# A four-layer selective scan on one core: instruction order in the scan stage taken from the source, with two steps issued one unit later

## The chip, the core and the metric

The kernel runs on one core of a Trainium2 chip. The core has five engines that run side by side: TensorE (PE, matrix multiplication), VectorE (DVE), ScalarE (ACT), GpSimd (POOL) and SyncE (SP), which here issues all the transfers between the chip's main memory and the core's own memory. An engine works through its own list of instructions and waits on semaphores for what other engines have to deliver. PE writes to PSUM[...]; everything else lies in the on-chip memory SBUF. The metric is the device time of one execution in microseconds (us). One execution was also taken by the profiler; all times by instruction come from it.

## The reference, cut to what matters

Four layers follow one another on eight images of 48 x 48 positions and 96 channels. Each adds to its input the result of a two-dimensional selective scan:

```
x = x + ss2d(groupnorm(x))          # four times, with different weights
ss2d: xz = x @ in_proj;  xc, z = halves of xz            # 192 channels each
      xc = silu(depthwise_conv3x3(xc))
      for each of 4 directions k (rows, columns, and both reversed), L = 2304 positions:
          dts, B, C = x_proj[k] @ xc                      # ranks 6 or 16, 16 states, 16 states
          delta = softplus(dt_proj[k] @ dts + bias)
          h[n]  = exp(delta * A[n]) * h[n] + delta * xc * B[n]      # along L, for n in 0..15
          y    += sum over n of h[n] * C[n]
      out = (layernorm(y) * silu(z)) @ out_proj
```

Layer 3 writes its scan as cumulative sums and a division by a decay. When the decay has faded to nothing, only the first and last positions matter, and the kernel computes just these ("short"), with a full second pass held in reserve.

## The kernel before, in words

**Tiling.** Two images form a pair, four pairs a layer, so layers 0 to 2 have twelve pairs. The 192 channels of both images are laid into three tiles of 128 partitions (t = 0 and 1 hold 128 channels of one image each, t = 2 the last 64 of both). A *group* is one tile t, one phase ph (rows or columns) and one direction d: twelve groups to a pair. A group's 2304 positions are scanned in three *chunks* of 768, each for 16 states n. One state of one chunk is a *unit*: 48 to a group, 576 to a pair, 6912 in layers 0 to 2.

**A unit**, in the class `Chunk`, has five steps:

- `load` (L518): SP fetches the row C[n], repeated over the partitions, into one of seven `cb` buffers, and for n = 0 also the rows of B (`brow`).
- `decay` (L537): ACT computes exp(delta * A[n]) into one of four `da` buffers (L543).
- `spread` (L548): PE spreads the row B[n] over the partitions into one of two PSUM tiles `b` (L558).
- `scan` (L562): DVE multiplies `b` by delta * u (L570) and scans (L574), in place in `da`. Unless the chunk is the last, ACT copies the last column of the scan into `carry` (L585), where the same state of the next chunk starts. Then POOL multiplies `cb` by the scan (L586).
- `add_up` (L588): PE adds `cb` into the single accumulator `acc` (L593). After n = 15 `collect` (L600) lets DVE add `acc` into y (L609, L614 or L619). At the end of a tile y is stored (L623).

**Side work.** Three generators are advanced in between, one step at a time, each step ending at a `yield`:

- `prepare` (L417) makes delta and delta * u of the next group, in five pieces of 480 or 384 positions. A piece has six steps: load of `dts` (L433); matmul and three ACT operations (L444 to L453); three ACT operations (L456 to L459); two POOL operations on `lg` (L461, L462); one DVE operation (L464); an ACT copy and a DVE product (L466, L468 or L470).
- `prologue` (L234) is the front end of the next pair: load of x (L310), group norm, input projection (L345, L352), the convolution as nine matmuls with diagonal weights per piece, three to a step (L258), silu with its table loads (L223, L224), x_proj (L395, L399), the store of its result (L411), and `split` (L270), which cuts it into three bf16 parts and stores them (L275 to L282). Its buffers `parts` and `rest` exist once.
- `epilogue` (L728) is layer norm, gate and output projection of the pair before, in 16 pieces of ten steps.

**The order of the work.** `run` (L839) writes one turn of a loop for each unit k: get_ready(k+1), which is load(k+3), decay(k+2) and spread(k+1); scan(k); one step of `prepare`; one step of `prologue` in the last third of a pair, or one of `epilogue` every second turn before that; add_up(k-3). This is the order of the source only. A planner inside the framework then decides the order in which each engine gets its instructions: it plays the program through with its own estimates of durations, and gives each engine, among the instructions that it takes to be ready, the one that stands first in the source. An instruction whose input it thinks late is passed by later ones. On the chip each engine keeps to the order that came out.

**Weights of a layer.** When a layer's first prologue begins, the constructor of `Layer` loads the weights and derives small tables from them (L178 to L197). `make_diag` (L200) then writes 18 diagonal matrices on DVE (L205), all at once.

Of the kernel before, what the change touches and what calls it, by code (L numbers as in the profile page):

```python
# [32 lines left out]
BF16 = mybir.dt.bfloat16  # L36
AF = mybir.ActivationFunctionType
ALU = mybir.AluOpType

P = 128  # L40
NB, H, W, DM = 8, 48, 48, 96
# [51 lines left out]
def ss2d_layers_kernel(ctx: ExitStack, tc: tile.TileContext, x_in, consts, weights, out):  # L93
    nc = tc.nc
# [47 lines left out]
    for b in range(2):  # L142
# [3 lines left out]
            mybir.AxisListType.X,  # L146
            ALU.add,
        )
# [7 lines left out]
    nc.vector.tensor_reduce(  # L156
        mine, ident.rearrange("p (b q) -> p b q", b=2), mybir.AxisListType.X, ALU.add
    )
# [4 lines left out]
    class Layer:  # L163


        def __init__(self, l):
            self.l = l
            self.rank = r = RANKS[l]
            self.nx = nx(r)
            cols, n = weight_columns(r)  # L170
            wt = wpool.tile([P, n], F32, name=f"w_{l}", tag="w")
            nc.sync.dma_start(wt, weights[l])
            part = {k: wt[:, a:b] for k, (a, b) in cols.items()}
            self.inw = part["inw"][0:DM]
            self.xp = part["xp"].rearrange("p (t f m) -> p t f m", t=2, f=2)
            self.dtw = part["dtw"].rearrange("p (k d) -> p k d", k=4)
            self.outw = part["outw"].rearrange("p (t c) -> p t c", t=2)
            self.outw_2 = wpool.tile([P, 2, DM], F32, name=f"outw2_{l}", tag="outw2")  # L178
            for b in range(2):
                nc.vector.tensor_scalar_mul(  # L180
                    self.outw_2[:, b, :], self.outw[:, 1, :], mine[:, b : b + 1]
                )
            self.par = part["par"].rearrange("p (t c) -> p t c", t=2)

            self.a = wpool.tile([P, 2, 4 * NS], F32, name=f"a_{l}", tag="a")
            nc.scalar.activation(self.a, self.par[:, :, C_ALOG : C_ALOG + 4 * NS], AF.Exp)
            nc.vector.tensor_scalar_mul(self.a, self.a, -1.0)

            self.amax = wpool.tile([P, 2, 4], F32, name=f"amax_{l}", tag="amax")
            nc.vector.tensor_reduce(  # L190
                self.amax, self.a.rearrange("p t (k n) -> p t k n", n=NS),
                mybir.AxisListType.X, ALU.max,
            )
            self.dsum = wpool.tile([P, 2], F32, name=f"dsum_{l}", tag="dsum")
            nc.vector.tensor_reduce(
                self.dsum, self.par[:, :, C_D : C_D + 4], mybir.AxisListType.X, ALU.add
            )  # L197
            self.diag = None

        def make_diag(self):  # L200

            self.diag = dpool.tile([P, 2, 9, P], F32, name=f"diag_{self.l}", tag="diag")
            for t in range(2):
                for j in range(9):
                    nc.vector.tensor_scalar_mul(  # L205
                        self.diag[:, t, j, :], ident, self.par[:, t, C_CONVW + j : C_CONVW + j + 1]
                    )

        def column(self, t, c):
            return self.par[:, int(t == 2), c : c + 1]  # L210
# [22 lines left out]

    def prologue(l, p, short=False):  # L234
        ly = layers[l]
        if ly.diag is None:
            ly.make_diag()
        gn = sm2.tile([DM, 2, 2], F32, name=f"gn_{l}_{p}", tag="gn")
        xd = dram.tile([2, 2, ly.nx, L], F32, name=f"xd_{l}_{p}", tag=f"xd{ly.rank}")
        xb = dram.tile([2, 2, PARTS, 3 * NS, L], BF16, name=f"xb_{l}_{p}", tag="xb")  # L240
# [4 lines left out]
        def padded(name):  # L245
            pad = tmp.tile([P, H + 2, W + 2], F32, name=name, tag="tmp")
            nc.gpsimd.memset(pad[:, 0 : H + 2 : H + 1, :], 0.0)
            nc.gpsimd.memset(pad[:, 1 : H + 1, 0 : W + 2 : W + 1], 0.0)
            return pad
# [20 lines left out]
        def split(xt, c0, m, to):  # L270
# [13 lines left out]
                )  # L284
            yield

        pad2 = padded(f"pad2_{l}_{p}")
        for b in range(2):
            x = tmp.tile([DM, L], F32, name=f"x_{l}_{p}_{b}", tag="tmp")
# [43 lines left out]
            nc.scalar.activation(scale, scale, AF.Exp, scale=-0.5)  # L333
            nc.vector.scalar_tensor_tensor(shift, mg, -1.0, scale, ALU.mult, ALU.mult)
            yield
# [165 lines left out]
    def picked(t, n):  # L501
# [2 lines left out]
            return 2 * NR, pick2[:, n, :]  # L504
        return NR, pick[:, n : n + 1].to_broadcast([NR, P])

    class Chunk:


# [52 lines left out]
        def scan(self, n):  # L562
            s, m = state[self.l, self.p], self.m
            way = (lambda z: z) if self.d == 0 else (lambda z: z[:, ::-1])
            _, du = s["dd", self.t, self.ph, self.d]
            carries = self.group["carry"]
            start = 0.0 if self.first else carries[:, n : n + 1]
            da, c = self.da.pop(n), self.cb[n][:, :m]
            b = self.b.pop(n)[:, :m]
            nc.vector.tensor_mul(b, du[:, self.c0 : self.c0 + m], b)  # L570
            if self.l < NLAYER - 1:

                h = da
                nc.vector.tensor_tensor_scan(way(h), way(da), way(b), start, ALU.mult, ALU.add)  # L574
            else:

                h = self.rq.pop(n)
                nc.vector.tensor_mul(b, h, b)
                nc.vector.tensor_tensor_scan(
                    way(h), ones.to_broadcast([P, m]), way(b), start, ALU.mult, ALU.add  # L580
                )
                nc.gpsimd.tensor_mul(c, c, da)
            if not self.last:
                end = m - 1 if self.d == 0 else 0
                nc.scalar.copy(carries[:, n : n + 1], h[:, end : end + 1])  # L585
            nc.gpsimd.tensor_mul(c, c, h)  # L586

        def add_up(self, n):  # L588
            if n == 0:
                self.acc = pacc.tile([P, 2 * BANK], F32, name="acc", tag="acc")  # L590
            c = self.cb.pop(n)
            for z, zm in pieces(self.m):
                nc.tensor.matmul(  # L593
                    self.acc[:, z : z + zm], ident, c[:, z : z + zm],
                    start=(n == 0), stop=(n == NS - 1),
                )
            if n == NS - 1:
                self.collect()

        def collect(self):  # L600

# [23 lines left out]
    class Edge:  # L625
# [68 lines left out]
        def add_up(self, i):  # L694
            if i == 0:
                self.acc = pacc.tile([P, 2 * BANK], F32, name="acc", tag="acc")
            c = self.cb.pop(i)
            for j in range(QUAD):
                nc.tensor.matmul(  # L699
                    self.acc[:, :EDGE], ident, c[:, j, :],  # L700
                    start=(i == j == 0), stop=(QUAD * i + j == NS - 1),
                )
            if QUAD * i + QUAD == NS:
                self.collect()

        def collect(self):
            l, p, t, s = self.l, self.p, self.t, state[self.l, self.p]
# [118 lines left out]
    def drain(g):  # L826
        for _ in g:
            pass

    def step(g, n=1):  # L830
        for _ in range(n):
            if next(g, StopIteration) is StopIteration:
                return

    groups = [(t, ph, d) for t in range(3) for ph in range(2) for d in range(2)]
    LAG = 3
    LOADS, DECAYS = 2, 1

    def run(pairs, short):  # L839
# [40 lines left out]
        drain(begin(*pairs[0]))  # L880
        drain(prepare(*pairs[0], *groups[0], pairs[0][0] in short))
        behind = ahead = coming = iter(())
        get_ready(0)
        for k, ((l, p, gi, j), c, n) in enumerate(todo):
            at = pairs.index((l, p))
            following = pairs[at + 1] if at + 1 < len(pairs) else None
            per = NS // QUAD if l in short else len(SCANS) * NS
            unit = gi * per + j

            after = 2 * len(groups) * per // 3  # L890
            if unit == after:
                drain(behind)
                if following:
                    ahead = begin(*following)
            if j == 0:
                drain(coming)
                if gi + 1 < len(groups):
                    coming = prepare(l, p, *groups[gi + 1], l in short)
                elif following:
                    drain(ahead)  # L900
                    coming = prepare(*following, *groups[0], following[0] in short)
                else:
                    coming = iter(())
            if j == max(0, per - 1 - LOADS - DECAYS):
                drain(coming)
            get_ready(k + 1)
            c.scan(n)
            step(coming)
            if unit >= after:
                step(ahead, 8 if l in short else 1)  # L910
            elif l in short:
                step(behind, 6)
            elif unit % 2 == 0:
                step(behind)
            if k >= LAG:
                todo[k - LAG][1].add_up(todo[k - LAG][2])
                (bl, bp, bgi, bj) = todo[k - LAG][0]
                if todo[k - LAG + 1][0][:2] != (bl, bp):
                    behind = epilogue(bl, bp)
        for (_, c, n) in todo[-LAG:]:  # L920
            c.add_up(n)
        drain(epilogue(*pairs[-1]))

    last = NLAYER - 1
    run([(l, p) for l in range(NLAYER) for p in range(NPAIR)], (last,))


    every = sm1.tile([P, 1], F32, name="every", tag="every")
# [102 lines left out]
```

## Time and profile before

| | |
|---|---|
| time, median of 3 runs | 25900.11 us (25893.95 to 25902.8) |
| span of the profiled execution | 25882.9 us |
| PE busy | 20983.2 us (81%) |
| DVE busy | 20922.0 us (81%) |
| POOL busy | 15340.0 us (59%) |
| ACT busy | 13772.3 us (53%) |
| DMA engines, mean share | 40.2% |

A row for a group of instructions gives the line, the engine, the operation, what it writes and reads, its shape and count; after the first bar the busy time in all and the mean of one in ns; after the second bar the time for which the engine stood idle just before such instructions, and the instruction whose end released it. A row of waits reads: who waited, for whom, us in total, how often, the longest. In the timeline the first number is the start in us, the second how long the instruction, or several alike in a row (x2, x4), took. A busy share is an average over stages that have different limits, so the stages of one pair are looked at apart.

### The profile page before, as it was taken

To read this page: it belongs to the slowest core of one execution; us is meant where nothing else is said; L and a number is where in the kernel's file an instruction comes from. 1 tells how busy PE (TensorE), PEld (TensorE's weight loads), DVE (VectorE), ACT (ScalarE), POOL (GpSimd) and SP (SyncE) were. 2 spreads that over 40 slices of the span, in tenths; PEclk is the share of its full clock that TensorE was granted. 3 is DMA by queue.
4 is the path that set the end of the run, shared out by engine and by line. 5 is a ranking of instruction groups with operands and counts; after the bars stand their busy time and mean duration, and the time that the engine had idled before them with its cause. 6 is when DMAs were issued, how large, how long until landed. Compare 5 with 4: busy or idle time off the path is not lost. (4 is left out here: it accounts for less than half of the span.)

```text
span 25882.9 us, 233918 instructions
## 1 busy us (share of the span) xinstructions
PE 20983.2 (81%) x64962; PEld 9542.0 (37%) x64962; DVE 20922.0 (81%) x18566; ACT 13772.3 (53%) x22878; POOL 15340.0 (59%) x9545
## 2 busy tenths in 40 slices
PE   7787887887887887887887887887887887887886
PEld 2333333333333333333333333333333333334555
DVE  5888888988888988988988988988888988887443
ACT  4454554554554554554554554554554554555775
POOL 4656656656666656656656656656656656655332
PEclk8898898998898898898898998898898998898886
DMA  2344444434434444434434444444434434444221
GB/s 90 126 122 130 132 123 127 134 119 130 134 120 132 135 121 133 134 121 134 134 121 131 134 122 130 134 121 130 134 119 132 134 120 130 132 122 115 64 62 50
DMA packets 1463442, 3150.92 MB, mean 122 GB/s; under 512 B 190832, under 2 KB 563696, under 8 KB 1448944
## 3 DMA queue, kind: packets, MB, share of 16 engines
q1 hardware_dynamic: 1462128, 3135.85, 40.2%
q8 instruction: 525, 8.60, 0.1%
q14 instruction: 789, 6.46, 0.1%
HBM read 2971.05 MB, written 164.07 MB: 121 GB/s over the span
## 5 line engine op out<-in xcount | busy, mean ns | idle before, releaser
L586 POOL TENSOR_TENSOR cb<-cb,da 128x768 f32<-128x768 f32 x6912 | 12427.8, 1809 | 7755.9 <-DVE da L574 4843.6
L593 PE MATMUL acc<-cb,cst 128*128 128x512 f32 (+1 forms) x27648 | 12228.8, 568 | 2394.0 <-POOL cb L586 2114.9
L543 ACT ACTIVATE da<-dl,a 128x768 f32<-128x768 f32 x6912 | 6448.9, 935 | 7878.0 <-POOL cb L586 7851.1
L570 DVE TENSOR_TENSOR b<-du,b 128x768 f32<-128x768 f32 x6912 | 6481.8, 951 | 2488.9 <-PE b L558 2461.6
L574 DVE TENSOR_TENSOR_SCAN da<-da,carry,b 128x768 f32<-128x768 f32 x4608 | 8182.2, 1801 | 90.0 <-ACT da L543 35.4
L593 PEld LDWEIGHTS acc<-cb,cst 128*128 128x128 f32 x27648 | 5323.8, 213 | 7776.8 <-issue 4049.3
L558 PE MATMUL b<-brow,pick 48*128 48x512 bf16 (+3 forms) x13824 | 3721.7, 354 | 1719.3 <-DVE da L574 1637.9
L574 DVE TENSOR_TENSOR_SCAN da<-da,b 128x768 f32<-128x768 f32 x2304 | 3961.5, 1742 | 83.1 <-ACT da L543 54.1
L558 PEld LDWEIGHTS <-pick 48*128 48x128 bf16 (+1 forms) x13824 | 919.9, 98 | 5287.6 <-DVE da L574 3139.0
L585 ACT COPY carry<-da 128x1 f32<-128x1 f32 x4608 | 847.4, 184 | 2226.7 <-DVE da L574 2205.3
L258 PE MATMUL ps<-pad,diag 128*128 128x480 f32 (+1 forms) x4320 | 1799.7, 559 | 60.2 <-ACT u L223 36.3
L461 POOL TENSOR_TENSOR lg<-lg,w 128x480 f32<-128x480 f32 (+2 forms) x768 | 864.8, 1126 | 837.5 <-ACT w L459 753.6
L464 DVE SCALAR_TENSOR_TENSOR ps<-ps,lg 128x480 f32<-128x480 f32 (+2 forms) x768 | 473.9, 617 | 799.3 <-POOL lg L462 756.3
L258 PEld LDWEIGHTS ps<-pad,diag 128*128 128x128 f32 x4320 | 783.2, 191 | 857.9 <-issue 619.9
L444 PE MATMUL ps<-dts,w 6*128 6x480 f32 (+8 forms) x2048 | 933.3, 628 | 73.9 <-DVE du L470 39.5
L744 PE MATMUL ps<-ey,cst 128*128 128x144 f32 (+1 forms) x4096 | 846.9, 334 | 82.4 <-ACT ey L768 66.5
L462 POOL TENSOR_TENSOR lg<-lg,e 128x480 f32<-128x480 f32 (+2 forms) x768 | 863.0, 1124 | 37.3
L745 PE MATMUL ps<-ey,mean 128*128 128x144 f32 (+1 forms) x4096 | 782.7, 315 | 0.0
L744 PEld LDWEIGHTS ps<-ey,cst 128*128 128x128 f32 (+1 forms) x4096 | 511.6, 179 | 364.9 <-issue 185.3
L448 ACT ACTIVATE ps<-ps,w 128x480 f32<-128x480 f32 (+2 forms) x768 | 457.7, 596 | 347.4 <-PE ps L444 346.8
L224 ACT ACT_TABLE_LOAD x496 | 636.4, 1283 | 8.7
L223 ACT ACT_TABLE_LOAD x496 | 636.4, 1283 | 8.2
(118 smaller groups left out, 14292.6 us busy)
## 6 DMA issues: line engine op xcount, KB each, us to landing
cb<-xd SPq DMA_DIRECT2D x4736, 384.0 KB
cb<-xd SPq DMA_DIRECT2D x4736, 192.0 KB
yd<-y SPq DMA_DIRECT2D x48, 1152.0 KB
ey<-yd SPq DMA_DIRECT2D x256, 216.0 KB
brow<-xb SPq DMA_DIRECT2D x576, 72.0 KB
xb<-parts SPq DMA_DIRECT2D x288, 108.0 KB
ex<-xs SPq DMA_DIRECT2D x256, 108.0 KB
xd<-xt SPq DMA_DIRECT2D x32, 684.0 KB
```

The source lines that it names most:

```text
L258: nc.tensor.matmul(ps[:, :m], ly.diag[:, int(t == 2), j, :], pad[:, r0 + dy : r0 + dy + nr, dx : dx + W], start=(j == 0), stop=(j == 8),)
L444: nc.tensor.matmul(o[:, :m], ly.dtw[q0 : q0 + r, k, chans], dts[q0 : q0 + r, :m], start=True, stop=True,)
L461: nc.gpsimd.tensor_sub(lg, lg, w1)
L462: nc.gpsimd.tensor_add(lg, lg, e)
L543: nc.scalar.activation(da, dl[:, self.c0 : self.c0 + m], AF.Exp, scale=columns_of(self.l, self.t, self.ph, self.d, n),)
L558: nc.tensor.matmul(b[:, z : z + zm], w, self.brow[:k, z : z + zm], start=True, stop=True)
L570: nc.vector.tensor_mul(b, du[:, self.c0 : self.c0 + m], b)
L574: nc.vector.tensor_tensor_scan(way(h), way(da), way(b), start, ALU.mult, ALU.add)
L585: nc.scalar.copy(carries[:, n : n + 1], h[:, end : end + 1])
L586: nc.gpsimd.tensor_mul(c, c, h)
L593: nc.tensor.matmul(self.acc[:, z : z + zm], ident, c[:, z : z + zm], start=(n == 0), stop=(n == NS - 1),)
L744: nc.tensor.matmul(o, mean_w[:, cols], z[:, b, :], start=True, stop=False)
```

## The change

`keep_order` adds, for every instruction between two marks, a dependency on the instruction before it on the same engine, without a semaphore. The planner then has to give each of the five engines its instructions in the order of the source. The marks enclose everything from the first `get_ready` to the first unit of layer 3, so the scans of layers 0 to 2 and the side work among them.

Two steps are issued later. `scan` no longer copies its last column: the copy is put on a list, and the next turn issues it after its `get_ready` and before its own scan. POOL's product now stands ahead of it. In the same way `collect` is put on a list by `add_up` and issued in the next turn, ahead of that turn's scan (in layer 3 as well).

The tables of a layer are no longer derived at once: `derive` is a part of the layer's first prologue, begun after four empty steps, and it ends a step after each small group of operations and after every third diagonal.

```diff
+ENGINES = (
+    mybir.EngineType.PE, mybir.EngineType.DVE, mybir.EngineType.Activation,
+    mybir.EngineType.Pool, mybir.EngineType.SP,
+)
...
+        def derive(self):
...
             self.outw_2 = wpool.tile([P, 2, DM], F32, name=f"outw2_{l}", tag="outw2")
...
+            yield
...
-        def make_diag(self):
...
             for t in range(2):
...
+                    if j % 3 == 2:
+                        yield
...
     def prologue(l, p, short=False):
         ly = layers[l]
-        if ly.diag is None:
-            ly.make_diag()
...
+        if ly.diag is None:
+            for _ in range(4):
+                yield
+            yield from ly.derive()
...
+    late_act, late_dve = [], []
+
+    def catch_up():
+        while late_dve:
+            late_dve.pop(0)()
+        while late_act:
+            nc.scalar.copy(*late_act.pop(0))
+
...
                 nc.gpsimd.tensor_mul(c, c, da)
+            nc.gpsimd.tensor_mul(c, c, h)
             if not self.last:
                 end = m - 1 if self.d == 0 else 0
-                nc.scalar.copy(carries[:, n : n + 1], h[:, end : end + 1])
-            nc.gpsimd.tensor_mul(c, c, h)
+                late_act.append((carries[:, n : n + 1], h[:, end : end + 1]))
...
             if n == NS - 1:
-                self.collect()
+                late_dve.append(self.collect)
...
+    def keep_order(a, b):
+
+        last = {}
+        info = mybir.DependencyInfo(mybir.DependencyClass.NoSync, mybir.DependencyReason.DATA)
+        for i in tc._region_blocks()[0].instructions[a:b]:
+            if i.engine in ENGINES:
+                if i.engine in last:
+                    tc.add_manual_dep(i, last[i.engine], info, reason="order")
+                last[i.engine] = i.name
...
+        mark()
         get_ready(0)
...
+            if l in short and unit == 0:
+                mark()
...
             get_ready(k + 1)
+            catch_up()
             c.scan(n)
...
         for (_, c, n) in todo[-LAG:]:
             c.add_up(n)
+            catch_up()
         drain(epilogue(*pairs[-1]))
...
+    keep_order(*marks[:2])
```

More of the change, by code (lines that the diff above doesn't have):

```diff
@@ L177, in __init__ @@
             self.outw = part["outw"].rearrange("p (t c) -> p t c", t=2)
+            self.par = part["par"].rearrange("p (t c) -> p t c", t=2)
+            self.diag = None
+        def derive(self):
+            l = self.l
             self.outw_2 = wpool.tile([P, 2, DM], F32, name=f"outw2_{l}", tag="outw2")
@@ L182, in __init__ @@
                 )
-            self.par = part["par"].rearrange("p (t c) -> p t c", t=2)
+            yield
             self.a = wpool.tile([P, 2, 4 * NS], F32, name=f"a_{l}", tag="a")
             nc.scalar.activation(self.a, self.par[:, :, C_ALOG : C_ALOG + 4 * NS], AF.Exp)
+            yield
             nc.vector.tensor_scalar_mul(self.a, self.a, -1.0)
@@ L197, in __init__ @@
             )
-            self.diag = None
-        def make_diag(self):
             self.diag = dpool.tile([P, 2, 9, P], F32, name=f"diag_{self.l}", tag="diag")
@@ L285, in split @@
             yield
+        if ly.diag is None:
+            for _ in range(4):
+                yield
+            yield from ly.derive()
         pad2 = padded(f"pad2_{l}_{p}")
@@ L703, in add_up @@
             if QUAD * i + QUAD == NS:
-                self.collect()
+                late_dve.append(self.collect)
         def collect(self):
@@ L833, in step, with mark @@
                 return
+    marks = []
+    def mark():
+        marks.append(len(tc._region_blocks()[0].instructions))
+    def keep_order(a, b):
[6 more added lines that the diff above has]
+                last[i.engine] = i.name
     groups = [(t, ph, d) for t in range(3) for ph in range(2) for d in range(2)]
```

## The prediction

> **What bounds the kernel now.** First the page's totals and costliest groups:
>
> ```profile
> PE 20983.2 (81%) x64962; PEld 9542.0 (37%) x64962; DVE 20922.0 (81%) x18566; ACT 13772.3 (53%) x22878; POOL 15340.0 (59%) x9545
> ...
> L570 DVE TENSOR_TENSOR b<-du,b 128x768 f32<-128x768 f32 x6912 | 6481.8, 951 | 2488.9 <-PE b L558 2461.6
> L574 DVE TENSOR_TENSOR_SCAN da<-da,carry,b 128x768 f32<-128x768 f32 x4608 | 8182.2, 1801 | 90.0 <-ACT da L543 35.4
> ```
>
> VectorE's product and scan of 6912 units (one state of one chunk each) are the spine; nearly all of its idle time there is a wait for PE's spread matmul L558. The waits by engine confirm it, and show a second kind:
>
> ```profile
> DVE b L570 <- PE b L558: 2461.6, 1879, 19.8
> DVE ps L464 <- POOL lg L462: 756.3, 308, 157.7
> ```
>
> Then busy time by stage, of the 8th image pair of the twelve in layers 0 to 2 (576 units; bounds by counting scans). The columns are the stretch, its length, busy us (instructions) of PE, PEld, DVE, ACT and POOL, granted clock, DMA share, GB/s:
>
> ```profile
> 14002.80:15233.60 1230.80, 1019.27 (x3168) 443.88 (x3168) 1109.96 (x949) 658.63 (x1098) 781.32 (x468) 0.89 0.43 134
> 15233.60:15271.90 38.30, 34.52 (x93) 14.58 (x92) 33.27 (x28) 19.92 (x38) 23.42 (x15) 0.87 0.41 127
> 15271.90:15516.70 244.80, 231.12 (x702) 108.88 (x701) 180.03 (x149) 150.05 (x224) 130.34 (x83) 0.99 0.36 108
> 15516.70:15633.90 117.20, 87.48 (x252) 35.72 (x250) 98.97 (x79) 53.74 (x93) 81.70 (x57) 0.91 0.51 134
> 15633.90:15796.80 162.90, 107.56 (x278) 41.61 (x276) 103.74 (x83) 70.84 (x119) 99.13 (x73) 0.82 0.45 118
> 15796.80:15952.60 155.80, 110.02 (x298) 48.55 (x298) 134.10 (x111) 68.09 (x115) 97.40 (x58) 0.85 0.43 128
> ```
>
> Stage A, units 0 to 383: 3.205 us a unit, DVE 90% busy. B: 12 units. C, 60 units with the next pair's convolutions: 4.08 each, PE 94% busy. D (two rows), 72 units with x_proj and split: 3.89, and no engine is full. E: 48 units, 3.25. Last, how DVE, PE and POOL pace one unit:
>
> ```profile
> 15513.03 0.95 DVE L570 TENSOR_TENSOR b<-du,b 128x768 f32<-128x768 f32 x1
> 15514.02 1.81 DVE L574 TENSOR_TENSOR_SCAN da<-da,carry,b 128x768 f32<-128x768 f32 x1
> 15515.75 0.94 DVE L570 TENSOR_TENSOR b<-du,b 128x768 f32<-128x768 f32 x1
> 15516.72 1.81 DVE L574 TENSOR_TENSOR_SCAN da<-da,carry,b 128x768 f32<-128x768 f32 x1
> 15518.45 1.80 DVE L570 TENSOR_TENSOR b<-du,b 128x768 f32<-128x768 f32 x2
> 15520.16 3.51 DVE L574 TENSOR_TENSOR_SCAN da<-da,carry,b 128x768 f32<-128x768 f32 x2
> 15523.59 1.80 DVE L570 TENSOR_TENSOR b<-du,b 128x768 f32<-128x768 f32 x2
> ```
>
> The planner often puts two products ahead of two scans: 5.14 us for two units, 2.57 each. Product and its own scan in turn take 2.70 to 2.72, and 2.78 where the scan starts 1.06 after its product (15501.61 to 15502.67).
>
> ```profile
> 15434.07 0.49 PE L558 MATMUL b<-brow,pick 96*128 96x512 bf16 x2
> 15434.40 2.58 PE L258 MATMUL ps<-pad,diag 128*128 128x480 f32 x6
> 15436.82 1.45 PE L593 MATMUL acc<-cb,cst 128*128 128x512 f32 x4
> 15438.11 0.49 PE L558 MATMUL b<-brow,pick 96*128 96x512 bf16 x2
> ```
>
> PE's true price for a unit with a convolution step: spread 0.33, convolution step 2.42, sum 1.29, together 4.04 us.
>
> ```profile
> 15642.99 1.20 POOL L461 TENSOR_TENSOR lg<-lg,w 128x480 f32<-128x480 f32 x1 [4.85 <-ACT w L459]
> 15644.27 1.20 POOL L462 TENSOR_TENSOR lg<-lg,e 128x480 f32<-128x480 f32 x1
> ```
>
> POOL's two lg operations start 1.28 apart and take 1.20 each; its product of a unit (L586) takes 1.81.
>
> **What the Trainium skill says.** "PSUM — Partial Sum Buffer", Engine vs sequencer instructions: the queues of ACT, DVE and POOL are strictly first in, first out, and matmuls start in program order; so the written order decides. The trace agrees: one late spread left DVE idle for 16.8 us. "VectorE: DVE Perf Modes", The DRAIN you can't avoid: an operation held by nothing starts before the pipe is empty; here 0.86 us after a product, against 0.97 to 1.06 where its own scan needs its result. "Perfetto Trace Analysis", Identifying the Most-Contended Engine: matmul busy time is a poor measure; here rows of 568 ns mean stand for issues 0.43 and 0.22 us apart (512 and 256 columns), so I price PE by spacing.
>
> **The change, part by part.**
>
> *Order.* Nothing is removed; lookahead is. PE's spread for unit k+1 comes ahead of all else in turn k and waits only for scan k-1, so it has a whole unit of 2.74 us for its 0.33 to 0.5; even with an epilogue step of about 1.8 and a dt projection of 1.0, PE stays within it. DVE's waits for L558 outside stage C go to about zero. ACT's decay runs about two units ahead, SP's load about 11 us ahead (landing 3.6 us by the semaphores in the trace), so both stay hidden.
>
> *DVE service*, strictly alternating: 2.74 a unit (between the 2.70 and 2.78 shown). Per group of 48: prepare's five L464 (0.53) and products (0.56 or 0.87) 6.1; three collects (rows 939 to 1491 ns) 3.4; epilogue 1.84 per 20 units in 320 of A's 384 units. A: 384 × 2.74 + 8 × 9.5 + 16 × 1.84 = 1158 us.
>
> *New wait at L464.* In turn k POOL does product k, then both lg operations; DVE's L464 is next after scan k+1. POOL starts 0.22 after a scan (14132.52 to 14132.74), then 1.80 + 1.28 + 1.20: ready at 4.50, DVE there at 2.74: wait 1.76, the 384-wide form 1.35. Per group 8.4, less 0.8 for other DVE work in between: 7.6. Behind it queue the next product and scan, and through them POOL and the second next spread. A: 8 × 7.6 = 61. Bounds: 0 if POOL is early, 3.57 each if POOL is one product behind.
>
> *A* = 1158 + 61 + 10 for DMA behind the 1.15 MB stores of y (estimate from their 4.7 us landing) = 1229 (now 1231). *B*: now twelve units carry five input projections in line: 47 (now 38), x's load (7.9 us) waited for. *C*: 45 convolution turns × (4.04 + 0.15 of dt) = 189, 15 others 52: 241 (now 245). L464's wait hides under PE here.
>
> *D*: 20 x_proj turns × 3.6 (PE) = 72; 48 split turns: parts and rest have one buffer, so cast, subtraction, cast, subtraction and store (0.5, 0.9, 0.5, 0.9, 2.0) plus one unit's product, 1.8, and waits ring in about 7.0 us per two turns: 168 (bounds 6.2, DVE's pace, to 8); four others 12: 252 (now 280). Now SP stands 22 us behind ACT for one store (L411) with loads queued behind it; in source order that store comes a turn after its copy. *E*: 48 × 2.94 + 7.6 + 2 = 151 (now 156).
>
> *Late column.* 4608 copies of 184 ns on ACT move behind the next decay and wait for a scan already finished; ACT is 53% busy: nothing. Products on POOL move ahead of them: at most the 407 us that POOL waits for ACT's column today, already in the stages. *Late collect*: DVE waits for sums issued a turn ago: nothing, except after a heavy PE turn; below 6 us a pair, inside A's margin. *derive*: 54 diagonals of 0.28 us inside the ordered part, spread over turns: about 0.
>
> Sum per pair: 1229 + 47 + 241 + 252 + 151 = 1920 against 1950: -30, ×12 = -360. Pairs 1 to 3 have a last third 20 us slower today: -60. The last pair has no D to gain: +30. Total -390. Layer 3 is outside the order. 25883 - 390 = 25493; the timed median is 17 above the profiled span: 25510.
>
> **Rivals.** (1) 0.10: L464's wait isn't there, since POOL or ACT hides it: 10.6 groups a pair outside C × 7.6 × 12 = 970 less: 24540. For: now only 756 us in all; against: two lg operations behind a product are 4.3 us, longer than a unit. (2) 0.30, slower: the same wait is longer, POOL being already behind when lg comes. 127 groups × 5 waits: beyond 0.61 us more each it eats the 390. A product (1.81) in three of four adds 860: 26370. For: stage A is two thirds of the time and has no reserve in my sum; against: POOL needs 1.8 of 2.74 us. (3) 0.05: the order on the chip is already the source's: 25900. Against: two products stand before two scans.
>
> **How the numbers follow.** The sum as worked out has 0.55: 25510, by itself 25200 to 25800. About 0.2% (50 us) is what a measurement can tell. Faster: 0.50 of the 0.55 and 0.10 of (1), with 0.01 of (3): 0.61. Same: 0.03 + 0.04: 0.07. Slower: 0.30 + 0.02: 0.32. The range takes in half of (2) beyond its point and stops short of (1)'s end: 24700 to 26450.
>
> **What would show it.** Right: product and scan strictly in turn on DVE; L570's wait for L558 below 1200 us and nearly all in C; L464's wait for L462 about 1000 to 1200 us; stage A unchanged within 1%, D shorter by 10%. Wrong: L464's wait near zero, or above 1700; DVE waiting for ACT's da in D (the ring above 8); L558 waiting for brow or dts loads in A.

## The result: 1.6% slower, and the profile after

| | before | after |
|---|---|---|
| time, median of 4 runs each | 25,897.03 us (25,888.06 to 25,902.8) | 26,308.86 us (26,269.74 to 26,319.41) |
| ratio after/before, 95% interval | | 1.0157 [1.0139, 1.0174] |
| span of the profiled execution | 25,882.9 us | 26,309.6 us |

The forecast was 25,510 us. The time is inside its range and on the wrong side of the kernel before. The page's totals and groups of after that answer to those shown of before:

```profile
PE 20485.2 (78%) x64962; PEld 9398.7 (36%) x64962; DVE 21418.1 (81%) x18566; ACT 13653.4 (52%) x22802; POOL 15438.2 (59%) x9545
...
L593 DVE TENSOR_TENSOR b<-du,b 128x768 f32<-128x768 f32 x6912 | 6552.2, 948 | 1127.4 <-PE b L581 1122.5
L597 DVE TENSOR_TENSOR_SCAN da<-da,carry,b 128x768 f32<-128x768 f32 x4608 | 8357.5, 1814 | 447.3 <-ACT da L566 13.2
L478 DVE SCALAR_TENSOR_TENSOR ps<-ps,lg 128x480 f32<-128x480 f32 (+2 forms) x768 | 481.8, 627 | 1192.9 <-POOL lg L476 1186.0
```

L593, L597, L581, L606, L616 and L478 are L570, L574, L558, L586, L593 and L464 of before. Idle time ahead of products is more than halved (2488.9 to 1127.4 us); ahead of scans (173 to 679 us over both forms) and of L478 it has grown. DVE is also busy for 496 us more. The waits by engine, of the whole run:

```profile
DVE ps L478 <- POOL lg L476: 1186.0, 686, 160.3
DVE b L593 <- PE b L581: 1122.5, 785, 7.7
```

About 246 us of the first row, and 242 of its 756.3 before, lie in layer 3, outside the changed order. In layers 0 to 2 the wait for `lg` goes from 514 to 940 us and the wait for the spread from 2,462 to 1,122.

One place in DVE's timeline shows the new wait, and the second fence is POOL's over the same stretch:

```profile
14300.36 1.81 DVE L597 TENSOR_TENSOR_SCAN da<-da,carry,b 128x768 f32<-128x768 f32 x1
14303.80 0.67 DVE L478 SCALAR_TENSOR_TENSOR ps<-ps,lg 128x480 f32<-128x480 f32 x1 [1.63 <-POOL lg L476]
14304.38 0.95 DVE L593 TENSOR_TENSOR b<-du,b 128x768 f32<-128x768 f32 x1
```

```profile
14299.53 1.81 POOL L606 TENSOR_TENSOR cb<-cb,da 128x768 f32<-128x768 f32 x1 [1.41 <-ACT w L473]
14301.30 1.20 POOL L475 TENSOR_TENSOR lg<-lg,w 128x480 f32<-128x480 f32 x1
14302.58 1.19 POOL L476 TENSOR_TENSOR lg<-lg,e 128x480 f32<-128x480 f32 x1
```

POOL starts on a unit's product 0.14 us after that unit's scan has ended (a scan from 14297.64 for 1.75; the releaser in the bracket is inferred, and the input that comes last is the scan), then does both `lg` operations; they are done at 14303.77, 4.4 us after that scan's end. DVE needs only one more product and scan, done at 14302.17, to arrive at L478. It stands there for 1.63 us with the next product queued behind it.

The stages of the 8th pair, bounded as before by counting scans (columns: stretch, length, busy us and instructions of PE, PEld, DVE, ACT and POOL, granted clock, DMA share, GB/s):

```profile
14247.30:15498.50 1251.20, 977.14 (x3164) 428.66 (x3163) 1132.16 (x937) 647.05 (x1080) 785.74 (x465) 0.91 0.42 131
15498.50:15556.60 58.10, 34.83 (x84) 14.18 (x82) 49.03 (x52) 22.17 (x40) 27.61 (x17) 0.79 0.43 132
15556.60:15810.40 253.80, 232.22 (x672) 108.64 (x673) 186.27 (x161) 144.26 (x218) 125.67 (x80) 0.94 0.35 101
15810.40:16083.30 272.90, 201.24 (x564) 84.40 (x563) 206.87 (x160) 127.33 (x220) 179.81 (x126) 0.88 0.44 126
16083.30:16252.80 169.50, 106.60 (x304) 46.19 (x303) 137.71 (x110) 72.37 (x122) 102.58 (x64) 0.88 0.40 119
```

This pair runs into a new layer: the derivation of the tables stands in its B, and the front end behind it comes later, so that three of its splits slip into E. The means over all twelve pairs, from the starts of the scans, are the better measure:

| us a pair | A | B | C | D | E | sum |
|---|---|---|---|---|---|---|
| before | 1230.9 | 38.3 | 248.3 | 278.8 | 155.4 | 1951.7 |
| predicted | 1229 | 47 | 241 | 252 | 151 | 1920 |
| after | 1253.3 | 59.8 | 257.3 | 258.7 | 157.0 | 1986.1 |

The row of the prediction is its sum for a pair like the 8th. Against before, only D has gained. A has lost 22 us a pair and B as much, and C nine. Twelve times +34.4 is 413 us of the 427 by which the two profiled spans differ; the rest of the program differs by 14.

The same 413 us by what DVE did in layers 0 to 2 (a wait is an idle time of more than 0.15 us; shorter gaps are counted with the busy time as DVE's service):

| us, layers 0 to 2 | before | after | difference |
|---|---|---|---|
| service of DVE | 20,017 | 21,030 | +1,013 |
| waits for the spread | 2,462 | 1,122 | -1,339 |
| waits for `lg` | 514 | 940 | +426 |
| waits for the sums that `collect` adds | 191 | 515 | +324 |
| other waits | 237 | 226 | -11 |

The waits together have fallen by 599 us. What outweighs that is the service: half of its growth is busy time, and half the short gaps between a product and its own scan.

### The profile page after: what moved, and what is told of

It reads as the page before. It is cut to its first block, busy times and chain, and to the rows that moved or that the text cites. A ratio compares the mean times of both kernels' runs of the same rounds, so it can differ in the third digit from the quotient of the medians.

```text
span 26309.6 us, 226116 instructions
## 1 busy us (share of the span) xinstructions
PE 20485.2 (78%) x64962; PEld 9398.7 (36%) x64962; DVE 21418.1 (81%) x18566; ACT 13653.4 (52%) x22802; POOL 15438.2 (59%) x9545
## 4 chain that ended last, share of the span: by engine, by line
DVE 47%; PE 29%; POOL 10%; issue 5%; DMA 4%; ACT 3%; SPq 1%; DVEq 0%; POOLq 0%; ACTq 0%
DVE da L597 27%; DVE b L593 14%; PE acc L616 10%; PE ps L268 6%; POOL cb L606 4%; PE b L581 3%; POOL lg L476 2%; POOL lg L475 2%; PE ps L458 2%; DMA dts<-xd 2%; PE ps L767 1%; DVE ps L478 1%; DVE y L642 1%; PE ps L768 1%; SPq L556 1%
## 5 line engine op out<-in xcount | busy, mean ns | idle before, releaser
L606 POOL TENSOR_TENSOR cb<-cb,da 128x768 f32<-128x768 f32 x6912 | 12527.9, 1813 | 8797.9 <-DVE da L597 5738.2
L616 PE MATMUL acc<-cb,cst 128*128 128x512 f32 (+1 forms) x27648 | 11775.1, 553 | 252.1 <-DVE y L642 107.3
L597 DVE TENSOR_TENSOR_SCAN da<-da,carry,b 128x768 f32<-128x768 f32 x4608 | 8357.5, 1814 | 447.3 <-ACT da L566 13.2
L616 PEld LDWEIGHTS acc<-cb,cst 128*128 128x128 f32 x27648 | 5193.6, 207 | 6590.7 <-issue 5836.5
L593 DVE TENSOR_TENSOR b<-du,b 128x768 f32<-128x768 f32 x6912 | 6552.2, 948 | 1127.4 <-PE b L581 1122.5
L581 PE MATMUL b<-brow,pick 48*128 48x512 bf16 (+3 forms) x13824 | 3704.4, 351 | 4369.8 <-DVE da L597 4099.5
L597 DVE TENSOR_TENSOR_SCAN da<-da,b 128x768 f32<-128x768 f32 x2304 | 4040.7, 1754 | 232.1 <-ACT da L566 28.3
L581 PEld LDWEIGHTS <-pick 48*128 48x128 bf16 (+1 forms) x13824 | 940.6, 98 | 6899.5 <-DVE da L597 5584.1
L478 DVE SCALAR_TENSOR_TENSOR ps<-ps,lg 128x480 f32<-128x480 f32 (+2 forms) x768 | 481.8, 627 | 1192.9 <-POOL lg L476 1186.0
L475 POOL TENSOR_TENSOR lg<-lg,w 128x480 f32<-128x480 f32 (+2 forms) x768 | 865.0, 1126 | 333.2 <-ACT w L473 333.1
L476 POOL TENSOR_TENSOR lg<-lg,e 128x480 f32<-128x480 f32 (+2 forms) x768 | 862.9, 1124 | 59.7
L480 ACT COPY dl<-ps 128x480 f32<-128x480 f32 (+2 forms) x768 | 404.6, 527 | 872.0 <-DVE ps L478 869.5
```

The lines of the kernel that those rows point to most:

```text
L475: nc.gpsimd.tensor_sub(lg, lg, w1)
L476: nc.gpsimd.tensor_add(lg, lg, e)
L581: nc.tensor.matmul(b[:, z : z + zm], w, self.brow[:k, z : z + zm], start=True, stop=True)
L616: nc.tensor.matmul(self.acc[:, z : z + zm], ident, c[:, z : z + zm], start=(n == 0), stop=(n == NS - 1),)
```

## The experiments

My theory after the result: the order gives a real gain, because DVE no longer waits for late spreads, and loses more at one place, L478, whose producer POOL comes directly ahead of it in the fixed order. The remaining loss is many small waits that the sum had at nothing. (The theory leaves out the dearer service of the table above.) The rival: the fixed order is bad as such, with strict alternation on DVE too dear. Times below are medians, and ratios are against the kernel before, measured beside each experiment (25,882 to 25,888 us).

### Without the order: is it the order that costs?

```diff
-    keep_order(*marks[:2])
```

> The changed kernel without keep_order: late columns, late collects and derive stay, the planner orders again. Theory (the order itself makes the kernel slower, by DVE's strict alternation of product and scan and by waits that the planner had stepped around): about as before, 25,900 us (25,800 to 26,000). Rival (the late columns and collects cost the time): near 26,300.

Measured: 25,861.48 us, ratio 0.9989 [0.9981, 0.9996]. Stages 1229.7, 36.6, 246.8, 280.1 and 156.4: those of before. DVE's waits in layers 0 to 2 are those of before too (531 us for `lg`, 2,434 for the spread), and so is its service (20,014 us). The late column, the late collect and the tables in steps cost nothing when the planner is free to place them. The whole loss comes with the order.

### One empty step between `lg` and its consumer

```diff
             nc.gpsimd.tensor_add(lg, lg, e)
             yield
+            yield
             nc.vector.scalar_tensor_tensor(v, v, 0.0, lg, ALU.max, ALU.add)
```

> The changed kernel with one empty step in prepare between the two lg operations on POOL and DVE's scalar_tensor_tensor, so that this comes a turn later. Theory (DVE's waits for lg are on the path and cost their full length): the wait of about 1000 us in layers 0 to 2 falls below 150 and the time falls by 800 to 950 us, to 25,350 to 25,500. Rival (while DVE waits, PE and the loads catch up, so other waits take its place): the wait goes all the same, and the time falls by less than 400 us, with DVE's waits for the spread matmul grown.

Measured: 25,365.5 us, ratio 0.9797 [0.978, 0.9813], 943 us below after. Its waits of DVE:

```profile
DVE b L594 <- PE b L582: 1093.5, 737, 8.6
...
DVE ps L479 <- POOL lg L476: 254.1, 48, 161.3
```

The 254.1 us left over are 245 of layer 3 and 8.8 in layers 0 to 2, against 940. The wait for the spread has hardly moved (1,122.5 to 1,093.5). So 931 us of wait removed gave 943 us of time: in the fixed order nearly every microsecond that DVE stood at L478 was on the path. This is the experiment that carries the theory. DVE's service stays as dear as in after (20,992 us); with the waits for `lg` gone, the time saved on the spreads is more than that costs.

### The product of the next unit ahead of the scan

The product of unit k+1 is issued before scan k, into a tile in SBUF, so that a scan doesn't have to await its own product.

```diff
+        def product(self, n):
...
+            q = qpool.tile([P, SCAN], F32, name="rq", tag="rq")[:, : self.m]
+            b = self.b.pop(n)[:, : self.m]
+            nc.vector.tensor_mul(q, du[:, self.c0 : self.c0 + self.m], b)
+            self.rq[n] = q
...
-            b = self.b.pop(n)[:, :m]
-            nc.vector.tensor_mul(b, du[:, self.c0 : self.c0 + m], b)
             if self.l < NLAYER - 1:
+                b = self.rq.pop(n)
...
+                if l < NLAYER - 1:
+                    c.product(n)
```

> The changed kernel with DVE's product of unit k+1 issued ahead of the scan of unit k, written to the SBUF buffers that layer 3 alone used, in layers 0 to 2; all else in the source's order. Theory (an alternating product and scan pay about 0.19 us each because the scan waits for its own product's result): 0.17 to 0.19 us less per unit, 1150 to 1300 us in all where DVE is the pace, so 25,050 to 25,300. Rival (with both operands in SBUF, DVE and POOL get in each other's way): scan or POOL's product becomes longer than 1.81 us and the gain is lost. Second rival (DVE isn't the pace, PE and waits are): under 400 us.

Measured: 30,405.47 us, ratio 1.1734 [1.1714, 1.1753]. The gap between product and scan is gone (0.86 to 0.88 us from one start to the next, against 1.05), and it doesn't help, since scan and `lg` operations have become slower:

```profile
L604 DVE TENSOR_TENSOR_SCAN da<-da,carry,rq 128x768 f32<-128x768 f32 x4608 | 10756.6, 2334 | 0.0
...
L475 POOL TENSOR_TENSOR lg<-lg,w 128x480 f32<-128x480 f32 (+2 forms) x768 | 1590.8, 2071 | 337.6 <-ACT w L473 337.5
```

The scan rises from 1814 to 2334 ns, `lg` from 1126 to 2071. The timelines show who holds up whom:

```profile
14351.07 1.20 POOL L475 TENSOR_TENSOR lg<-lg,w 128x480 f32<-128x480 f32 x1
14352.35 2.62 POOL L476 TENSOR_TENSOR lg<-lg,e 128x480 f32<-128x480 f32 x1
```

```profile
14352.23 1.75 DVE L604 TENSOR_TENSOR_SCAN da<-da,rq 128x768 f32<-128x768 f32 x1
14355.01 0.67 DVE L478 SCALAR_TENSOR_TENSOR ps<-ps,lg 128x480 f32<-128x480 f32 x1 [1.03 <-POOL lg L476]
```

L475 ran beside almost no scan (0.04 us) and took 1.20. L476 began 0.12 after a scan and ended 0.99 after the scan's end: it can have done little while the scan ran. The Trainium skill, "SBUF — State Buffer", Who interferes with whom, says that a VectorE instruction with two inputs in SBUF and a GpSimd instruction that reads SBUF exclude each other. This trace agrees (1.20 against 2.62 us). In the kernel before and in after, `b` lies in PSUM and the scan is left alone. The rival named for this run held, and the gap of 0.2 us a unit stays; it wasn't tried with the product left in PSUM. The slower instructions aren't all of the loss: DVE's waits for the spread are 2,490 us here against 1,122 in after, and PE is at half clock (see below) for 10,906 us against 5,848.

### The order for all engines but DVE

```diff
 ENGINES = (
-    mybir.EngineType.PE, mybir.EngineType.DVE, mybir.EngineType.Activation,
+    mybir.EngineType.PE, mybir.EngineType.Activation,
```

> The changed kernel with keep_order for PE, ACT, POOL and SP, while the planner orders DVE alone. Theory (DVE's alternation and DVE's place of the lg operation are what costs): products stand in twos again or lg's consumer later, DVE busy falls by several hundred us, time 25,500 to 26,000. Rival (the fixed order of the other engines is what costs, in the stretches with the next pair's front end): near 26,300 with the waits for PE unchanged.

Measured: 25,646.38 us, ratio 0.9904 [0.9888, 0.9921]. In layers 0 to 2 the wait for `lg` is longer than in after (1,093 us) and the one for the spread lies between before and after (1,518). A is 1212.0. DVE's waits together are no shorter than in after (2,846 us against 2,804). What falls is its service, from 21,030 to 20,317 us: in places the planner goes back to two products before two scans (1,054 times, 2,074 before). So the theory's first half holds, the alternation costs; that the place of L478 costs as well doesn't show here, since the wait for `lg` stays. The order of the other four engines alone gains 1.0% on before.

### Column and collect at once

The order stays, but the last column and the sums' collection are issued where they were.

```diff
-            nc.gpsimd.tensor_mul(c, c, h)
...
-                late_act.append((carries[:, n : n + 1], h[:, end : end + 1]))
+                nc.scalar.copy(carries[:, n : n + 1], h[:, end : end + 1])
+            nc.gpsimd.tensor_mul(c, c, h)
...
-                late_dve.append(self.collect)
+                self.collect()
```

> The changed kernel with the last columns and the collects issued at once, as before the change, but in the source's order. Theory (in a fixed order ACT would then stand until the scan just issued is done, and DVE until the sums just issued are done): slower than the changed kernel, by 200 to 1200 us, 26,500 to 27,500, with ACT's wait of the column for the scan near 6000 us. Rival (ACT has enough lead and lateness buys nothing): within 100 us of 26,300.

Measured: 26,785.93 us, ratio 1.035 [1.0333, 1.0367]. ACT's waits for its carry copies, first of after and then of this kernel:

```profile
ACT carry L528 <- DVE da L597: 1083.5, 1422, 3.7
```

```profile
ACT carry L608 <- DVE da L597: 7074.9, 3230, 5.5
```

ACT stands behind the scan with decay and the steps of `prepare` queued; DVE's wait for ACT's copy of delta (L482 and L484) grows to 578 us. The two late steps save about 480 us once the order is fixed, and without the order nothing (first experiment). They belong to the order.

### The order for DVE alone

```diff
 ENGINES = (
-    mybir.EngineType.PE, mybir.EngineType.DVE, mybir.EngineType.Activation,
-    mybir.EngineType.Pool, mybir.EngineType.SP,
+    mybir.EngineType.DVE,
 )
```

> The changed kernel with keep_order for DVE alone; the planner orders PE, ACT, POOL and SP. Theory (strict alternation costs DVE 0.08 to 0.15 us a unit, and the waits for PE's late spreads stay as they were before): DVE busy rises by 400 to 500 us against the kernel without keep_order, time 26,200 to 26,800. Rival (alternation gives PE a whole unit for its spread and so takes its waits away, whatever orders PE): about 25,900 or below.

Measured: 25,444.1 us, ratio 0.9832 [0.9815, 0.9848]. My theory had this slower than before; the rival was right.

```profile
DVE ps L477 <- POOL lg L475: 1071.3, 246, 156.0
DVE b L592 <- PE b L580: 878.0, 653, 10.0
```

In layers 0 to 2 strict alternation makes DVE busy for 411 us more than before, adds 546 us of short gaps, and takes 1,556 us off the waits for the spread (2,434 without the order, to 878). The wait for `lg` is there (833 us in layers 0 to 2), but in 200 places instead of 641. With the planner setting the order of POOL, `lg` mostly comes early enough, and now and then very late (19.3 us at most).

### The empty step, with DVE left to the planner

```diff
-    mybir.EngineType.PE, mybir.EngineType.DVE, mybir.EngineType.Activation,
+    mybir.EngineType.PE, mybir.EngineType.Activation,
...
             nc.gpsimd.tensor_add(lg, lg, e)
             yield
+            yield
```

> Both at once: one empty step behind the lg operations, and DVE ordered by the planner while PE, ACT, POOL and SP keep the source's order. Theory (the wait for lg, 943 us, and DVE's alternation, 663 us, are separate costs): the two gains add, 24,600 to 24,850. Rival (they are in part the same time: with products in twos the spread of PE comes just in time and its waits return): 25,100 to 25,400.

Measured: 25,484.52 us, ratio 0.9841 [0.9823, 0.9859]. Neither the theory's sum nor the rival's range was met; the two cures don't add. Where DVE is free, the step leaves 779 us of the wait for `lg` in layers 0 to 2 (1,093 without it), where the full order had 8.8: the planner seems to move L478 forward again. The waits for the spread are 1,663 us.

### The empty step, and slack for the loads too

Beside the step after `lg`, one more empty step after the load of `dts` and two after the load of x:

```diff
                 nc.sync.dma_start(x, src[b])
+                yield
+                yield
...
             yield
+            yield
...
             nc.gpsimd.tensor_add(lg, lg, e)
             yield
+            yield
```

> The kernel with the empty step behind lg (25,365 us), with one more empty step between the load of dts and its matmul and two more behind the load of x. Theory (in line PE and DVE stand for transfers that the planner stepped around: PE 281 us for dts, DVE for x): the two waits all but vanish, 150 to 350 us less, 25,000 to 25,200, most of it in the twelve units at the start of the next pair's front end and in the split stretch. Rival (PE has slack enough there): within 60 us of 25,365.

Measured: 25,309.17 us, ratio 0.9778 [0.9761, 0.9794], the lowest median of the study. PE's wait for `dts` falls from 281 to 100 us, yet the time falls by 56 us only against the single empty step, and the two intervals overlap: the rival's figure was met. PE's slack isn't all of the reason. DVE's waits for the spread fell too, from 1,094 to 778 us, but its waits for the sums that it collects grew, from 502 to 735 us over the three forms of `collect`, and those for ACT's copy of delta from 168 to 212: most of the wait came back at other places.

### The empty step, with the order for DVE alone

```diff
-    mybir.EngineType.PE, mybir.EngineType.DVE, mybir.EngineType.Activation,
-    mybir.EngineType.Pool, mybir.EngineType.SP,
+    mybir.EngineType.DVE,
...
             nc.gpsimd.tensor_add(lg, lg, e)
             yield
+            yield
```

> DVE alone in the source's order, with the empty step behind the lg operations. Theory (DVE's wait for lg, about 850 us in layers 0 to 2 of that kernel, is idle time on the path whoever orders POOL): 24,700 to 25,000. Rival (PE's waits or other ones take its place, or the planner, which sets POOL's place of lg, moves lg back as well): within 200 us of 25,444.

Measured: 25,492.24 us, ratio 0.9849 [0.9832, 0.9865], no gain over the DVE order without the step. The wait for `lg` falls from 833 to 693 us only, and the wait for the spread grows from 878 to 1,100. POOL's order is the planner's here, and the slack given in the source seems to be mostly gone on the chip; the rival had named both.

### The empty step without any order

```diff
             nc.gpsimd.tensor_add(lg, lg, e)
             yield
+            yield
...
-    keep_order(*marks[:2])
```

> No fixed order at all, with the empty step behind the lg operations. Theory (the gap heals only what the fixed order brought; the planner had already moved the consumer of lg back): within 150 us of 25,861. Rival (the gap helps the kernel whatever its order): 25,300 to 25,500.

Measured: 25,545.49 us, ratio 0.9871 [0.9854, 0.9887]. The step gains 316 us without the order too, against the theory and a little less than the rival had it, though the wait for `lg` falls from 531 to 450 us only and the wait for the spread from 2,434 to 2,145. So part of what order_lg_gap gains on before isn't due to the order.

### More matmuls: is it PE's clock or PE's load?

In stage A the late spreads of after go together with PE's clock at half (next section). If low activity makes the clock fall, more matmuls would raise it and shorten the waits. The last 256 columns of each spread are issued twice; nothing else is changed.

```diff
-            for z, zm in pieces(self.m):
+            for z, zm in pieces(self.m)[1:] + pieces(self.m):
```

> The kernel in fixed order with the empty step behind lg (25,365 us), where PE spreads the last 256 columns of each unit twice (the first result is overwritten): about 0.1 to 0.2 us more PE work per unit, 700 to 1400 us in all. Theory (PE's clock falls to half when PE is idle in part, and spreads are late because of that): half-clock time falls from 4423 us to below 3000, DVE's wait for the spread doesn't grow, time within 150 us of 25,365 or below it. Rival (PE's load itself makes the spreads late): the wait grows by 300 us or more and the time by 200 to 700 us.

Measured: 25,831.91 us, ratio 0.9975 [0.9967, 0.9983], 466 us above the same kernel without the doubled piece.

```profile
DVE b L594 <- PE b L582: 1460.9, 985, 8.3
```

Time at half clock went up, from 4,423 to 5,053 us, and the wait for the spread from 1,093.5 to 1,460.9. So more matmuls don't keep the clock up here, and another 256 columns a unit are enough to lengthen the waits by 367 us. The run doesn't part load from clock, since both went up: in the twelve stages A the wait grew from 146 to 422 us, and 421 of these 422 us had some half clock in the 5.4 us before the product. What makes the clock fall stays open.

### The orders side by side

Ratio to before, with and without the empty step:

| the fixed order holds for | no empty step | one empty step after `lg` |
|---|---|---|
| no engine | 0.9989 | 0.9871 |
| DVE alone | 0.9832 | 0.9849 |
| all but DVE | 0.9904 | 0.9841 |
| all five (the change) | 1.0157 | 0.9797 |

The order on all five is the worst of the left column and the best of the right one. The alternation on DVE alone is worth 1.6%. Fixing the other engines as well puts POOL's `lg` in front of DVE without slack, and one step of slack takes 3.6% off that.

## Why the prediction was wrong

**What it had right.** Product and scan stand strictly in turn (6,902 of 6,912 scans directly behind their product; two products before two scans 2,074 times before, never now). DVE's wait for the spread is 1,122.5 us, below the 1,200 named, though only 411 of it lies in C, where nearly all of it was to be. The wait at L478 is there, by the mechanism and near the price given: 940 us in layers 0 to 2 against 970 worked out, 56 us in a stage A against 61. That the totals are so close is in part luck, since 65 us of the 940 lie in C, where it was to hide under PE; outside C it is 875. The single empty step shows that it is on the path. D is shorter, by 7% and not 10%: 258.7 us against 252. Its ring was priced well: two splits start 7.5 us apart in the median, where 7.0 was worked out (9.1 before). Rival 2, which held the other side, gave the wrong reason: the wait isn't longer than priced, and POOL isn't a product behind. Rivals 1 and 3 fell. The time lies inside the range only because half of this rival's side was taken in.

**What failed.** The sum credited the order with 390 us net where it costs 427. Stage A was to stay within 1% and is 1.8% longer. The gap of 66 us a pair is spread over all five stages: A +24, B +13, C +16, D +7, E +6. The step at fault is the one that says "DVE's waits for L558 outside stage C go to about zero", and with it "Late collect: ... nothing", with "below 6 us a pair" for heavy turns. Measured, the waits for the spread outside C are 711 us, 59 a pair (A 21, B 6, D 31, E 1), and those for the sums 515 us, 43 a pair (11, 5, 19, 4 and 5 in A to E; 16 before). The waits of DVE in stage A of the 8th pair:

```profile
DVE ps L478 <- POOL lg L476: 52.3, 36, 1.7
DVE b L593 <- PE b L581: 19.3, 17, 2.6
DVE y L642 <- PE acc L616: 5.6, 4, 2.1
DVE y L637 <- PE acc L616: 3.5, 2, 1.9
DVE y L632 <- PE acc L616: 3.1, 2, 1.9
```

The late spreads that were to be zero are 19.3 us here, the late collects 12.2. The means of the twelve stages A close the account. Against the 1229 of the prediction: service +6 (1164 where 1158 was worked out), `lg` -5, spreads +21, collects +11, other waits +1, and -10 for the DMA that was added as an estimate and has no wait of its own in the list; together the +24.

**Why the spread can be late with a unit's time in hand.** The prediction priced PE by the spacing of matmuls taken from a place with the clock at 0.99, and asked whether one turn's work fits into 2.74 us. At half the clock (granted 0.50 from 14330 to 14340), in after:

```profile
14332.86 1.64 PE L458 MATMUL ps<-dts,w 16*128 16x384 f32 x2 [0.29 <-DMA dts<-xd]
14334.44 2.93 PE L616 MATMUL acc<-cb,cst 128*128 128x512 f32 x4
14337.30 0.82 PE L581 MATMUL b<-brow,pick 48*128 48x512 bf16 x2
```

```profile
14338.15 0.96 DVE L593 TENSOR_TENSOR b<-du,b 128x768 f32<-128x768 f32 x1 [0.97 <-PE b L581]
14339.22 1.81 DVE L597 TENSOR_TENSOR_SCAN da<-da,carry,b 128x768 f32<-128x768 f32 x1
14342.90 0.96 DVE L593 TENSOR_TENSOR b<-du,b 128x768 f32<-128x768 f32 x1 [1.87 <-PE b L581]
```

The four matmuls of one unit's sum stand in front of the spread and take 2.93 us, where the prediction's fence of before had 1.45; the spread takes 0.82 for 0.49. With one dt projection ahead of them PE needs 5.3 us, nearly two turns of DVE. The granted clock was already 0.89 in A of before, shown in the prediction's own table and not used.

Counted over all twelve stages A of after, each of the 222 late spreads (248 us) had some half clock in the 5.4 us before its product, and also in the 5.4 us before the wait began. Of the 2,959 products without any, none came late. In before, 501 of the 1,149 late spreads of A had none. So the claim that one turn is enough for PE holds in A where the clock is full, and fails where it is at half. Half clock alone isn't enough: of the 1,649 products of after with some in those 5.4 us, one in seven was late; in the timeline a heavy turn comes on top, but the turns weren't counted by their weight. This is a count and no experiment, since no run set the clock. In C it is otherwise: 299 of its 339 late spreads had full clock throughout the 5.4 us, so PE's load is enough there. C holds 411 us of the 1,122, D 375 (339 of them with some half clock) and B 70.

**B.** Predicted 47, found 59.8: 72 in the first three pairs, whose next pair is of layer 0 and has its x loaded and transposed in pieces, and 54 to 58 in the others. The same three pairs have a C of 272 us against 252.5 in the others, which is 5 of C's 16; what the rest of C's excess is made of stays open. In the 8th pair, where the first prologue of layer 2 begins, PE's matmul for `dts` waited 3.91 us for a load issued 2.6 us behind the 908 KB of the layer's weights, and the diagonals are dearer than "about 0":

```profile
L215 DVE TENSOR_SCALAR diag<-cst,w 128x128 f32<-128x128 f32 x18 | 12.5, 749 | 0.0
```

749 ns is their mean; the median is 277, and six of the 18 took 1.56 to 1.84 us, each begun while one of POOL's products ran. The prediction's 0.28 was the median of before. There the 18 that lie among the units took 492 to 523 ns on average, so the steps add 4 to 5 us where a layer begins.

**Why A got longer at all.** Of the 1230.9 us of A in before, 120 were waits, 100 of them for the spread and 14 for `lg`, so service was 1111. Strict order adds 53 us of service and takes 80 off the spread's waits; the waits for `lg` add 42, the collects 11, and 5 go from the waits for ACT's copy of delta. That makes +21, where +22 was measured. The prediction had both sides of this, the dearer pace and the saved wait. It took the saved wait to be all of it, and so left nothing for the 31 us a pair of small waits in A, nor for their like in B, C, D and E.

## What to carry to other kernels

When an order written by hand takes the place of a planner's, check each consumer against its producer's queue and not its latency alone: POOL needed 4.4 us from a scan's end to have `lg` ready, DVE was there one product and one scan (2.8 us) later, and one empty step between them was worth 3.6%. Price the alternation itself too: here it cost DVE 1,013 us of service and saved 1,339 of waits. A step that looks free because it fits into a turn has to be priced with the clock that the stage is granted and with two heavy steps in one turn. And slack in the source counts most where the order of the source holds: the same empty step gained 3.6% in the fixed order and 1.2% in the planner's.

## What the hardware showed that I had not expected

- A scan with both inputs in SBUF and POOL's operations on `lg` shut each other out: an `lg` operation of 1.20 us that began beside a scan took 2.62, and the mean scan rose from 1.81 to 2.33 us. With `b` in PSUM the same scan kept 1.81 us beside POOL.
- PE's granted clock takes two values only in these traces, 1.0 and 0.5; the Trainium skill, "TensorE: Matmul & The Clock Gate", What's actually happening, names the same two. PE is at half for 6,142 us of before, 5,848 of after, and 4,423 with the empty step, in the middle of a program that keeps PE about 80% busy. Doubling the last third of each spread did not lower it (5,053).
- VectorE's small multiply of a diagonal by a column took 0.26 to 0.28 us in 36 of the 54 cases among the units of after. The other 18 had begun 0.15 to 0.33 us after one of POOL's products (two inputs in SBUF); they took 1.56 to 1.84 us and ended 0.08 or 0.09 us after that product.
